# Normalization statistics as matrix products beside the router logits, in a fused attention and mixture-of-experts layer

## The chip, the cores and the metric

The kernel runs on one core of a Trainium2 chip. The metric is the device time of one execution in microseconds (us), lower is better. A core has five engines with instruction streams of their own: TensorE (PE in the profile; its weight loads are listed as PEld), VectorE (DVE), ScalarE (ACT), GpSimd (POOL) and SyncE (SP), which here issues the loop's DMAs. They wait for one another by semaphores. SBUF is the working memory, PSUM holds what TensorE writes.

## The reference

The input x is [2, 128, 256, 256] in float32: two images, 128 channels, 65,536 pixels each. One layer is computed:

```python
x = x + conv(_ln_c(x), W_qkv, W_out, rel_height, rel_width)
t = _to_tokens(x)                       # a pixel is a token of 128 channels
t = t + ffn(_ln_t(t), router_w, router_b, expert_w, expert_b)
x = _from_tokens(t, x)

def _ln_t(v, eps=1e-5):                 # _ln_c: the same over channels, eps=1e-6
    m = mean(v, -1); s = var(v, -1)
    return (v - m) / sqrt(s + eps)

def ffn(x, ...):                        # E = 8 experts, the best 2 of each token
    router_probs = softmax(x @ router_w + router_b)
    top_p, top_i = top_k(router_probs, 2)
    top_p = top_p / sum(top_p)
    expert_out = einsum('bnd,edc->bnec', x, expert_w) + expert_b
    return einsum('bnk,bnkc->bnc', top_p, gathered expert_out)
```

`conv` is attention in windows of 8 x 8 queries and 12 x 12 overlapping keys, four heads of 32 channels, with relative-position logits and a fixed mask. The mask leaves a query only the keys whose row and column have its own parity. So the image falls apart into four planes (the four parities), and each plane is attended to by itself.

## The kernel before, in words

**Layout and stages.** Channels lie on the 128 partitions, pixels along the free dimension. The image is cut into strips of 8 rows (`R`), 64 strips for both images. A strip has four planes of 4 x 128 pixels, so 512 queries each. The main loop (L707) goes over 256 planes, and eight more turns to drain. A turn n does for plane n: the scores (`scores`), the softmax and values (`attend`), the output projection (`out_project`); for plane n + 1 the projections of q, keys and values (`project`). Beside this it does for one chunk f of 512 tokens of the strip before (two rows) the statistics of the second norm and the routing (`norms`, `route`, `spread`), for one chunk c of a coming strip the statistics of the first norm (`norms`), and for the chunk whose gates were spread a turn before the eight experts' products (`Experts`).

**Order.** The loop stands under `tc.manual_schedule`, so each engine runs its instructions in the order in which the Python code emits them. The helpers are generators; every `next(...)` emits one part. A turn emits, in this order: `norm` (statistics and raw logits), the first part of `score`, `norm`'s rest, `route`'s first part, `ahead` (q of the next plane, `pq`), `ahead` (`pu`, whose transpose uT is written by DVE), `route`, the `shift` of uT (two copies and a transpose to `au`, DVE), expert product 0, the second half of the scores, `ahead` (keys, `pk`), `route`'s end, products 1 and 2, the attention's first half, `spread`, product 3, `ahead` twice (values, `pvv`), the attention's second half and its end (DVE: sT, rc, rT, o), products 4 to 7, the output projection `po` and its add to xt (L498), the product with the experts' biases (L639) and its add to xt (L640).

**The statistics before.** `stats` (L219) transposes a chunk by four PE transposes into a PSUM tile `px`, so that tokens lie on partitions, and takes `bn_stats` of each 128 x 128 block on DVE. That is done for f (`px_f`) and for c (`px_c`). `rstd` (L228) merges the halves of bn_stats by five small DVE ops and makes 1/sqrt(variance + eps) as exp(-0.5 ln(...)) by two ACT ops, followed by a correction step on DVE.

**The logits before.** `plt` (L517): four products with the router's weights `rw`, padded to 32 columns, as stationary operand and 128 tokens of the chunk moving; product t writes partitions 32t to 32t + 31. ACT copies the result to SBUF (`lT`, L525), and in `route` a PE transpose (`plg`, L548) puts tokens on partitions. A float32 product is two matmul instructions in the profile (two passes), a transpose is one.

**Gates.** `spread` transposes the gates g (`pg`, L590), copies them (ACT, `gT`), and SP writes them to DRAM (`gd`) and reads them back spread over all partitions: `rb` for the first norm, and eight `gb` of 256 KB for the experts (L598, L617), whose multiplications by xt (`xe`, L628) are shared by DVE and POOL.

**PSUM.** `mm_tile` hands out three buffers in turn (`ps_mm`), shared by px, plt, plg, pq, pu, pk, pvv, pg and po. `att` and `acc` have tiles of their own.

`ln1_now` (L289) runs `norms` for a single chunk c with nothing else around it, eight times in all (before the loop and at the start of the second image).

Of the kernel before, what the change touches and what calls it, by code (L numbers as in the profile page):

```python
# [10 lines left out]
F32 = mybir.dt.float32  # L11
AF = mybir.ActivationFunctionType
ALU = mybir.AluOpType
# [3 lines left out]
P = 128  # L17
HEADS, DH = 4, 32
E = 8
SCALE = DH ** -0.5  # L20
CONV_EPS, FFN_EPS = 1e-6, 1e-5
# [26 lines left out]
def kernel(  # L48
# [39 lines left out]
    def mm_tile(name):  # L88
        return ps_mm.tile([P, 512], F32, tag="mm", name=name)

    def ctile(shape, name):
        return const.tile(shape, F32, tag=name, name=name)
# [49 lines left out]
    def centred(w, n, name):  # L142

        pm = mm_tile(f"pm_{name}")
        nc.tensor.matmul(pm[:, :n], lhsT=onesm, rhs=w, start=True, stop=True)
        nc.vector.tensor_sub(w, w, pm[:, :n])
# [5 lines left out]
    rw = ctile([P, 32], "rw")  # L152
    nc.vector.memset(rw, 0.0)
    nc.scalar.dma_start(rw[:, 0:E], router_w)
    centred(rw, 32, "rw")
# [47 lines left out]
    epsc = ctile([P, 2 * NT], "epsc")  # L203
    nc.vector.memset(epsc[:, 0:NT], C * FFN_EPS)
    nc.vector.memset(epsc[:, NT:], C * CONV_EPS)
# [13 lines left out]
    def stats(src, st, name):  # L219


        px = mm_tile(f"px_{name}")
        for t in range(NT):
            nc.tensor.transpose(px[:, t * P : (t + 1) * P], src[:, t * P : (t + 1) * P], ident)  # L224
        for t in range(NT):
            nc.vector.bn_stats(st[:, t, :], px[:, t * P : (t + 1) * P])

    def rstd(st, eps, n, name):  # L228

        u = small.tile([P, 2 * NT], F32, tag="u", name=f"u_{name}")[:, 0:n]
        d = small.tile([P, 2 * NT], F32, tag="d", name=f"d_{name}")[:, 0:n]
        r = small.tile([P, 2 * NT], F32, tag="r", name=f"r_{name}")[:, 0:n]
        nc.vector.tensor_tensor(d, st[:, 0:n, 1], st[:, 0:n, 4], ALU.subtract)
        nc.vector.tensor_tensor(u, st[:, 0:n, 2], st[:, 0:n, 5], ALU.add)
        nc.vector.scalar_tensor_tensor(d, d, C / 4.0, d, ALU.mult, ALU.mult)
        nc.vector.tensor_tensor(u, u, eps, ALU.add)
        nc.vector.tensor_tensor(u, u, d, ALU.add)  # L240
        nc.scalar.activation(r, u, AF.Ln, scale=4.0 / C)
        nc.scalar.activation(r, r, AF.Exp, scale=-0.5)
        yield
        nc.vector.scalar_tensor_tensor(u, u, -4.0 / C, r, ALU.mult, ALU.mult)
        nc.vector.tensor_tensor(u, u, r, ALU.mult)
        yield r, u
# [158 lines left out]
    def scores(n, state):  # L405
# [35 lines left out]
        pT = work.tile([P, HEADS, HQ], F32, tag="pT", name=f"pT{n}")  # L441
# [59 lines left out]
    def norms(f, c, nm):  # L501

        st = small.tile([P, 2 * NT, 6], F32, tag="st", name=f"st{nm}", bufs=4)
        g = small.tile([P, (2 * E + 1) * NT], F32, tag="g", name=f"g{nm}")
        n0, n1 = (0 if f else NT), (2 * NT if c else NT)
        rs = lT = None
        if f:
            src = rows_of(*f)  # L510
            stats(src, st, f"f{nm}")
        if c:
            stats(ln1_src(*c), st[:, NT:, :], f"c{nm}")
        if f:
            plt = mm_tile(f"plt{nm}")
            for t in range(NT):
                nc.tensor.matmul(  # L517
                    plt[32 * t : 32 * t + 32, :P],
                    lhsT=rw,
                    rhs=src[:, t * P : (t + 1) * P],  # L520
                    start=True,
                    stop=True,
                )
            lT = work.tile([P, P], F32, tag="lT", name=f"lT{nm}")
            nc.scalar.copy(lT, plt[:, :P])  # L525
        parts = rstd(st[:, n0:], epsc[:, n0:n1], n1 - n0, nm)
        next(parts)
        yield
        r, u = next(parts)
        if f:  # L530
            rs = small.tile([P, NT], F32, tag="rs", name=f"rs{nm}")
            nc.vector.scalar_tensor_tensor(rs, u[:, 0:NT], 3.0, r[:, 0:NT], ALU.add, ALU.mult)
        if c:
            nc.vector.scalar_tensor_tensor(
                g[:, 2 * NT * E :], u[:, NT - n0 :], 3.0, r[:, NT - n0 :], ALU.add, ALU.mult
            )
        yield g, rs, lT

    def rows_of(i, k):
        return xt[i][:, 2 * k : 2 * k + 2, :].rearrange("p r c -> p (r c)")  # L540

    def route(i, k, g, rs, lT):
# [4 lines left out]
        plg = mm_tile(f"plg{nm}")  # L547
        nc.tensor.transpose(plg[:, :P], lT, ident)  # L548
        p3 = plg[:, :P].rearrange("p (t e) -> p t e", e=32)[:, :, 0:E]
        lg = small.tile([P, NT, E], F32, tag="lg", name=f"lg{nm}")  # L550
        by_e = [P, NT, E]
        nc.vector.tensor_tensor(lg, p3, rs.broadcast_to(by_e), ALU.mult)
# [153 lines left out]
    with tc.manual_schedule(engines={ET.PE, ET.DVE, ET.Activation, ET.Pool, ET.SP}):  # L706
        for n in range(n_planes + 8):  # L707
# [17 lines left out]
            next(score, None)  # L725
            made = next(norm, None)
            if f:
                g, rs, lT = made
                rout = route(*f, g, rs, lT)
            next(rout, None)  # L730
            next(ahead, None)
            next(ahead, None)
            next(rout, None)
            if n + 1 < n_planes:
                states[n + 1]["shift"]()
# [24 lines left out]
            next(attn, None)  # L760
            ex.product(4)
# [77 lines left out]
```

## Time and profile before

| | |
|---|---|
| median of 3 runs | 5080.68 us (5078.29 to 5091.52) |
| the profiled execution, its time | 5112.45 us |
| its span, first to last instruction | 5110.7 us |
| mean granted clock of TensorE | 0.987 |
| PE busy | 4958.1 us, 97% of the span |
| DVE, ACT, POOL busy | 75%, 24%, 25% |
| bytes moved by DMA | 764.01 MB, mean 149 GB/s |

The profile is a record of one execution with the start and length of each instruction. Its page lists the engines' busy time, the DMA queues, the chain of work that ended last (followed back from the last instruction) and the costliest groups of instructions. Further views are a timeline by engine, the waits (who waited for whom) and tables by stretches of time. Lengths of matmuls contain the end of the pipeline, so neighbours overlap; the distance from one start to the next is what a matmul takes of PE's time. "issue" is time in which an engine waited for nothing that the profile shows.

### The profile page before, as it was taken

Reading aid. Unit: us, or ns where it says so; the run is one execution under the profiler, and the core shown is the slowest. Engines: PE = TensorE matmul, PEld = TensorE weight load, DVE = VectorE, ACT = ScalarE, POOL = GpSimd, SP = SyncE. Lnnn points to the kernel's source line nnn. Section 1 sums busy time; section 2 is a strip of 40 time slices with the busy share of each in tenths; the row PEclk is TensorE's granted clock in tenths of the full one; section 3 lists DMA queues with packets and bytes.
Section 4 is the critical chain, followed back from the end, with each engine's and each line's share of the span. In section 5 each row is a group of like instructions: output and inputs, shape, how many; then the busy total and the mean of one; then the engine's idle time right before and its main releaser. Section 6 shows DMA issues by size and latency. Waiting matters only on the chain.

```text
span 5110.7 us, 212340 instructions
## 1 busy us (share of the span) xinstructions
PE 4958.1 (97%) x93250; PEld 2962.2 (58%) x93250; DVE 3829.9 (75%) x11636; ACT 1236.3 (24%) x3021; POOL 1283.0 (25%) x1550
## 2 busy tenths in 40 slices
PE   5999999999999999999999999999999999999998
PEld 4555655555555555555555555565555555555554
DVE  5777777777777777777777777777777777777776
ACT  2222222222222222222222222222222222222221
POOL 2222222222222222222222222222222222222221
PEclk8999999999999999999999999999999999999999
DMA  1454545445454444545445444544545545454444
GB/s 51 130 156 150 159 149 160 148 152 167 149 152 154 154 153 148 155 153 157 140 141 167 148 153 151 157 159 147 161 144 156 156 152 152 148 167 147 145 143 148
DMA packets 375143, 764.01 MB, mean 149 GB/s; under 512 B 42850, under 2 KB 61898, under 8 KB 357834
## 3 DMA queue, kind: packets, MB, share of 16 engines
q1 hardware_dynamic: 371712, 749.36, 47.2%
q8 instruction: 733, 12.01, 0.9%
q14 instruction: 192, 1.57, 0.1%
q10 hardware_dynamic: 2506, 1.07, 0.1%
HBM read 674.25 MB, written 76.01 MB: 147 GB/s over the span
## 4 chain that ended last, share of the span: by engine, by line
PE 96%; issue 2%; DVE 2%; DMA 0%; ACT 0%; POOL 0%; SPq 0%; ACTq 0%; DVEq 0%; POOLq 0%
PE acc L633 35%; PE pvv L387 9%; PE att L434 8%; PE att L465 6%; PE pk L362 5%; PE pu L350 4%; PE pq L340 4%; PE po L493 4%; PE acc L639 4%; PE att L417 3%; PE att L455 3%; PE px_f L224 2%; PE px_c L224 2%; PE plt L517 2%; PE plg L548 1%
## 5 line engine op out<-in xcount | busy, mean ns | idle before, releaser
L633 PE MATMUL acc<-xe,ew 128*128 128x512 f32 x4096 | 1961.7, 602 | 1.8 <-DVE xt L640 1.7
L628 POOL TENSOR_TENSOR xe<-xt,gb 128x512 f32<-128x512 f32 x512 | 638.0, 1267 | 3715.4 <-PE acc L633 3690.4
L633 PEld LDWEIGHTS acc<-xe,ew 128*128 128x128 f32 x4096 | 748.4, 193 | 761.1 <-issue 683.1
L628 DVE TENSOR_TENSOR xe<-xt,gb 128x512 f32<-128x512 f32 x1536 | 948.8, 685 | 15.5 <-PE acc L633 15.0
L434 PEld LDWEIGHTS att<-qs,kcol 32*64 32x64 f32 x32768 | 430.0, 130 | 257.8 <-issue 257.1
L387 PEld LDWEIGHTS pvv<-wt,xcol 128*128 128x128 f32 x4096 | 498.7, 192 | 119.2 <-issue 119.0
L498 DVE TENSOR_TENSOR xt<-po,xt 128x512 f32<-128x512 f32 x256 | 177.2, 692 | 494.9 <-PE po L493 494.9
L434 PE MATMUL att<-qs,kcol 32*64 32x32 f32 x32768 | 466.4, 224 | 55.3 <-issue 54.8
L387 PE MATMUL pvv<-wt,xcol 128*128 128x128 f32 x4096 | 500.6, 275 | 0.0
L525 ACT COPY lT<-plt 128x128 f32<-128x128 f32 x256 | 68.1, 266 | 1716.5 <-PE plt L517 1716.5
L465 PEld LDWEIGHTS att<-pT,vv 64*32 64x32 f32 x32768 | 376.2, 106 | 69.1 <-issue 1.3
L475 DVE STREAM_TRANSPOSE sT<-att 128x512 f32<-128x512 f32 x256 | 183.5, 717 | 305.0 <-PE att L465 305.0
L394 ACT COPY vv<-pvv 128x512 f32<-128x512 f32 x512 | 300.1, 586 | 454.9 <-PE pvv L387 454.9
L465 PE MATMUL att<-pT,vv 64*32 64x32 f32 x32768 | 399.9, 199 | 0.2 <-issue 0.2
L282 POOL TENSOR_TENSOR xn<-xt,rb 128x512 f32<-128x512 f32 x248 | 372.8, 1503 | 61.9 <-DMA rb<-gd 61.9
L442 ACT ACTIVATE pT<-att 128x1024 f32<-128x1024 f32 x256 | 262.5, 1025 | 179.1 <-PE att L434 179.1
L362 PE MATMUL pk<-xn,wt 128*128 128x512 f32 (+2 forms) x528 | 291.7, 637 | 0.0
L493 PE MATMUL po<-o,wt 128*128 128x512 f32 x512 | 265.7, 601 | 16.9 <-DVE o L485 16.9
L340 PE MATMUL pq<-xn,wt 128*128 128x512 f32 x512 | 271.8, 613 | 6.8 <-DVE lg L556 2.6
L329 DVE STREAM_TRANSPOSE au<-auT 128x512 f32<-128x512 f32 x256 | 269.9, 1054 | 8.8
L350 PE MATMUL pu<-xn,wrel 128*128 128x512 f32 x512 | 271.2, 611 | 2.3 <-issue 1.4
L639 PE MATMUL acc<-ge,eb 128*128 128x512 f32 x512 | 261.5, 592 | 0.0
(2951 smaller groups left out, 5364.4 us busy)
## 6 DMA issues: line engine op xcount, KB each, us to landing
gb<-gd SPq DMA_DIRECT2D x2048, 256.0 KB
xt<-in_x_dram SPq DMA_DIRECT2D x64, 1024.0 KB
out_dram<-xt SPq DMA_DIRECT2D x64, 1024.0 KB
rb<-gd SPq DMA_DIRECT2D x248, 256.0 KB
gd<-gT SPq DMA_DIRECT2D x244, 34.0 KB
ge<-gd SPq DMA_DIRECT2D x256, 16.0 KB
ew<-in_L_ffn_expert_w_dram ACTq DMA_DIRECT2D x1, 512.0 KB
gd<-gT SPq DMA_DIRECT2D x12, 32.0 KB
```

Source lines behind the costliest of these rows:

```text
L282: eng.tensor_tensor(xn[i % 2][:, :, :, k, 1 : PC + 1], ln1_src(i, k).rearrange("p (y j x) -> p y x j", y=2, x=2), rb.rearrange("p (y j x) ...
L340: nc.tensor.matmul(pq, lhsT=wq, rhs=inner, start=True, stop=True)
L350: nc.tensor.matmul(pu, lhsT=wrel, rhs=inner, start=True, stop=True)
L362: nc.tensor.matmul(pk[:, : m * PC], lhsT=wk, rhs=xp[:, part[0] : part[0] + m, 1 : PC + 1], start=True, stop=True,)
L387: nc.tensor.matmul(pv[:, t * P : (t + 1) * P], lhsT=xl[:, t0 + t].rearrange("p a k -> p (a k)"), rhs=wv, start=True, stop=True,)
L394: nc.scalar.copy(vv[:, t0 : t0 + 4, :].rearrange("p t c -> p (t c)"), pv)
L434: nc.tensor.matmul(sc[rows, h, 32 * t : 32 * t + 32], lhsT=kk[hp, half * HP + t, :], rhs=qs[hp, m0 : m0 + 2].rearrange("p m a s -> p (m a ...
L465: nc.tensor.matmul(av[hp, half, 32 * t : 32 * t + 32], lhsT=vv[rows, t, hp], rhs=pT[rows, h, 32 * t : 32 * t + 32], start=True, stop=True,)
L493: nc.tensor.matmul(po, lhsT=wo, rhs=state["o"].rearrange("p f z -> p (f z)"), start=True, stop=True)
L628: eng.tensor_tensor(self.xe[e], self.src, self.gb.pop(e), ALU.mult)
L633: nc.tensor.matmul(self.acc, lhsT=ew[:, e, :], rhs=self.xe.pop(e), start=(e == 0), stop=False)
L639: nc.tensor.matmul(self.acc, lhsT=eb, rhs=self.ge, start=False, stop=True)
```

## The change

The transposes, bn_stats and half of `rstd` go. For each chunk ACT writes the squares of the raw values (`sq0`, `sq2`). The router's weights become four blocks of 32 columns: block 0 has the logits' weights, and block j has in column E + j the value 1/C (block 0 has its own too). Four times four products are accumulated in the same tile `plt`: block 0 with f, block 1 with f's squares, block 2 with c, block 3 with c's squares. So the columns after the eight logits hold the mean and the mean square of f and of c. After the copy `lT` and the transpose `plg`, which moves from `route` to `norms`, DVE reads the moments from PSUM, and `rstd` forms the variance as mean square less squared mean.

In the order of a turn: the squares are emitted first, then the first part of the scores, then the 16 products and `lT`, then q's projection (`pq`), then `plg` and `rstd`, then `route` and `pu`. The `shift` moves from before expert product 0 to after the attention's end (o), before product 4. pT and the squares have one buffer each.

```diff
--- before.py
+++ after.py
@@ -149,10 +149,14 @@
     nc.scalar.dma_start(ew, expert_w.rearrange("e d c -> d e c"))
     for e in range(0, E, 4):
         centred(ew[:, e : e + 4, :].rearrange("p e c -> p (e c)"), 512, f"ew{e}")
-    rw = ctile([P, 32], "rw")
+
+
+    rw = ctile([P, 4, 32], "rw")
     nc.vector.memset(rw, 0.0)
-    nc.scalar.dma_start(rw[:, 0:E], router_w)
-    centred(rw, 32, "rw")
+    nc.scalar.dma_start(rw[:, 0, 0:E], router_w)
+    centred(rw[:, 0, 0:E], E, "rw")
+    for j in range(4):
+        nc.vector.memset(rw[:, j, E + j : E + j + 1], 1.0 / C)
     rb = ctile([P, E], "rb")
     nc.scalar.dma_start(rb, router_b.partition_broadcast(P))
 
@@ -200,9 +204,9 @@
         nc.gpsimd.memset(auT[i][:, :, :, KR + 6 : KR + 7], NEG)
 
 
-    epsc = ctile([P, 2 * NT], "epsc")
-    nc.vector.memset(epsc[:, 0:NT], C * FFN_EPS)
-    nc.vector.memset(epsc[:, NT:], C * CONV_EPS)
+    epsc = ctile([P, 2, NT], "epsc")
+    nc.vector.memset(epsc[:, 0], FFN_EPS)
+    nc.vector.memset(epsc[:, 1], CONV_EPS)
 
 
     xn, xcol, kcol = [], [], []
@@ -216,34 +220,25 @@
         nc.gpsimd.memset(kcol[i], 0.0)
 
 
-    def stats(src, st, name):
-
-
-        px = mm_tile(f"px_{name}")
-        for t in range(NT):
-            nc.tensor.transpose(px[:, t * P : (t + 1) * P], src[:, t * P : (t + 1) * P], ident)
-        for t in range(NT):
-            nc.vector.bn_stats(st[:, t, :], px[:, t * P : (t + 1) * P])
-
-    def rstd(st, eps, n, name):
-
-
-
-
-        u = small.tile([P, 2 * NT], F32, tag="u", name=f"u_{name}")[:, 0:n]
-        d = small.tile([P, 2 * NT], F32, tag="d", name=f"d_{name}")[:, 0:n]
-        r = small.tile([P, 2 * NT], F32, tag="r", name=f"r_{name}")[:, 0:n]
-        nc.vector.tensor_tensor(d, st[:, 0:n, 1], st[:, 0:n, 4], ALU.subtract)
-        nc.vector.tensor_tensor(u, st[:, 0:n, 2], st[:, 0:n, 5], ALU.add)
-        nc.vector.scalar_tensor_tensor(d, d, C / 4.0, d, ALU.mult, ALU.mult)
-        nc.vector.tensor_tensor(u, u, eps, ALU.add)
-        nc.vector.tensor_tensor(u, u, d, ALU.add)
-        nc.scalar.activation(r, u, AF.Ln, scale=4.0 / C)
+    def rstd(p4, k0, k1, name):
+
+
+
+        u, r = (
+            small.tile([P, 2, NT], F32, tag=v, name=f"{v}_{name}")[:, k0:k1] for v in ("u", "r")
+        )
+        mean, sq = (
+            p4[:, :, E + 2 * k0 + j : E + 2 * k1 : 2].rearrange("p t k -> p k t") for j in range(2)
+        )
+        nc.vector.tensor_copy(r, mean)
+        nc.vector.tensor_tensor(u, r, r, ALU.mult)
+        nc.vector.scalar_tensor_tensor(u, u, -1.0, sq, ALU.mult, ALU.add)
+        nc.vector.scalar_tensor_tensor(u, u, 0.0, epsc[:, k0:k1], ALU.max, ALU.add)
+        nc.scalar.activation(r, u, AF.Ln, scale=4.0)
         nc.scalar.activation(r, r, AF.Exp, scale=-0.5)
-        yield
-        nc.vector.scalar_tensor_tensor(u, u, -4.0 / C, r, ALU.mult, ALU.mult)
+        nc.vector.scalar_tensor_tensor(u, u, -4.0, r, ALU.mult, ALU.mult)
         nc.vector.tensor_tensor(u, u, r, ALU.mult)
-        yield r, u
+        return r, u
 
     def ln_rows(i):
 
@@ -438,7 +433,7 @@
                         start=False,
                         stop=(t == HP - 1),
                     )
-        pT = work.tile([P, HEADS, HQ], F32, tag="pT", name=f"pT{n}")
+        pT = work.tile([P, HEADS, HQ], F32, tag="pT", name=f"pT{n}", bufs=1)
         nc.scalar.activation(pT, att[:, :, 0:HQ], AF.Exp)
         state.update(att=att, pT=pT)
         yield
@@ -502,54 +497,54 @@
 
 
 
-        st = small.tile([P, 2 * NT, 6], F32, tag="st", name=f"st{nm}", bufs=4)
         g = small.tile([P, (2 * E + 1) * NT], F32, tag="g", name=f"g{nm}")
-        n0, n1 = (0 if f else NT), (2 * NT if c else NT)
-        rs = lT = None
-        if f:
-            src = rows_of(*f)
-            stats(src, st, f"f{nm}")
-        if c:
-            stats(ln1_src(*c), st[:, NT:, :], f"c{nm}")
-        if f:
-            plt = mm_tile(f"plt{nm}")
+        srcs = []
+        for j, src in ((0, f and rows_of(*f)), (2, c and ln1_src(*c))):
+            if src is None:
+                continue
+            sq = work.tile([P, CH], F32, tag=f"sq{j}", name=f"sq{j}{nm}", bufs=1)
+            nc.scalar.activation(sq, src, AF.Square)
+            srcs += [(j, src), (j + 1, sq)]
+        yield
+        plt = mm_tile(f"plt{nm}")
+        for j, src in srcs:
             for t in range(NT):
                 nc.tensor.matmul(
                     plt[32 * t : 32 * t + 32, :P],
-                    lhsT=rw,
+                    lhsT=rw[:, j],
                     rhs=src[:, t * P : (t + 1) * P],
-                    start=True,
-                    stop=True,
+                    start=(j == srcs[0][0]),
+                    stop=(j == srcs[-1][0]),
                 )
-            lT = work.tile([P, P], F32, tag="lT", name=f"lT{nm}")
-            nc.scalar.copy(lT, plt[:, :P])
-        parts = rstd(st[:, n0:], epsc[:, n0:n1], n1 - n0, nm)
-        next(parts)
-        yield
-        r, u = next(parts)
+        lT = work.tile([P, P], F32, tag="lT", name=f"lT{nm}")
+        nc.scalar.copy(lT, plt[:, :P])
+        yield
+        plg = mm_tile(f"plg{nm}")
+        nc.tensor.transpose(plg[:, :P], lT, ident)
+        p4 = plg[:, :P].rearrange("p (t e) -> p t e", e=32)
+        k0, k1 = (0 if f else 1), (2 if c else 1)
+        r, u = rstd(p4, k0, k1, nm)
+        rs = None
         if f:
             rs = small.tile([P, NT], F32, tag="rs", name=f"rs{nm}")
-            nc.vector.scalar_tensor_tensor(rs, u[:, 0:NT], 3.0, r[:, 0:NT], ALU.add, ALU.mult)
+            nc.vector.scalar_tensor_tensor(rs, u[:, 0], 3.0, r[:, 0], ALU.add, ALU.mult)
         if c:
             nc.vector.scalar_tensor_tensor(
-                g[:, 2 * NT * E :], u[:, NT - n0 :], 3.0, r[:, NT - n0 :], ALU.add, ALU.mult
+                g[:, 2 * NT * E :], u[:, 1 - k0], 3.0, r[:, 1 - k0], ALU.add, ALU.mult
             )
-        yield g, rs, lT
+        yield g, rs, p4
 
     def rows_of(i, k):
         return xt[i][:, 2 * k : 2 * k + 2, :].rearrange("p r c -> p (r c)")
 
-    def route(i, k, g, rs, lT):
+    def route(i, k, g, rs, p4):
 
 
         nm = f"{i}_{k}"
         rs = rs.unsqueeze(2)
-        plg = mm_tile(f"plg{nm}")
-        nc.tensor.transpose(plg[:, :P], lT, ident)
-        p3 = plg[:, :P].rearrange("p (t e) -> p t e", e=32)[:, :, 0:E]
         lg = small.tile([P, NT, E], F32, tag="lg", name=f"lg{nm}")
         by_e = [P, NT, E]
-        nc.vector.tensor_tensor(lg, p3, rs.broadcast_to(by_e), ALU.mult)
+        nc.vector.tensor_tensor(lg, p4[:, :, 0:E], rs.broadcast_to(by_e), ALU.mult)
         nc.vector.tensor_tensor(lg, lg, rb.unsqueeze(1).broadcast_to(by_e), ALU.add)
         mx = small.tile([P, NT, 1], F32, tag="mx2", name=f"mx2{nm}")
         nc.vector.tensor_reduce(mx, lg, AX.X, ALU.max)
@@ -723,16 +718,14 @@
 
             next(norm, None)
             next(score, None)
+            next(norm, None)
+            next(ahead, None)
             made = next(norm, None)
             if f:
-                g, rs, lT = made
-                rout = route(*f, g, rs, lT)
+                rout = route(*f, *made)
             next(rout, None)
             next(ahead, None)
-            next(ahead, None)
             next(rout, None)
-            if n + 1 < n_planes:
-                states[n + 1]["shift"]()
             ex.product(0)
             next(score, None)
             next(ahead, None)
@@ -758,6 +751,8 @@
             next(ahead, None)
             next(attn, None)
             next(attn, None)
+            if n + 1 < n_planes:
+                states[n + 1]["shift"]()
             ex.product(4)
             ex.product(5)
             for e in (5, 7):
```

## The prediction

> **What bounds the kernel now.** I read the page first: engines, DMA queues and the chain that ended last.
>
> ```profile
> span 5110.7 us, 212340 instructions
> PE 4958.1 (97%) x93250; PEld 2962.2 (58%) x93250; DVE 3829.9 (75%) x11636; ACT 1236.3 (24%) x3021; POOL 1283.0 (25%) x1550
> ...
> q8 instruction: 733, 12.01, 0.9%
> ...
> PE 96%; issue 2%; DVE 2%; DMA 0%; ACT 0%; POOL 0%; SPq 0%; ACTq 0%; DVEq 0%; POOLq 0%
> ```
>
> TensorE (PE) carries 96% of the chain, "issue" 2%. So the change is worth what it does to PE's own time, to those issue gaps, and to any new PE wait. Next the timeline of PE over one undisturbed plane (start, length, work):
>
> ```profile
> 2727.86 0.60 PE L224 MATMUL px_f<-ident,xt 128*128 128x128 f32 x4
> 2728.29 0.60 PE L224 MATMUL px_c<-ident,xt 128*128 128x128 f32 x4
> 2728.82 0.43 PE L517 MATMUL plt<-xt,rw 128*32 128x128 f32 x8
> 2729.18 0.69 PE L417 MATMUL att<-au,keys 32*64 32x128 f32 x32
> 2729.67 0.90 PE L434 MATMUL att<-qs,kcol 32*64 32x32 f32 x64
> 2730.50 0.33 PE L548 MATMUL plg<-ident,lT 128*128 128x128 f32 x1
> 2730.66 1.02 PE L340 MATMUL pq<-xn,wt 128*128 128x512 f32 x2
> 2731.53 1.02 PE L350 MATMUL pu<-xn,wrel 128*128 128x512 f32 x2
> 2732.39 1.02 PE L633 MATMUL acc<-xe,ew 128*128 128x512 f32 x2
> 2733.34 0.86 PE L434 MATMUL att<-qs,kcol 32*64 32x32 f32 x64
> ...
> 2738.09 0.30 PE L590 MATMUL pg<-ident,g 128*68 128x128 f32 x1
> ...
> 2746.91 0.60 PE L224 MATMUL px_f<-ident,xt 128*128 128x128 f32 x4
> ```
>
> Lengths include the pipeline's end; what a piece costs is the distance between starts. The plane takes 2746.91 - 2727.86 = 19.05 us, the median of all planes, with no hole. Third, PE's waits, and the chain in order of time and the table of stretches around one of them:
>
> ```profile
> PE att L434 <- issue: 54.8, 54, 2.7
> ```
>
> ```profile
> 2527.67 0.60 PE att L417 x30
> 2528.27 0.55 PE att L434 x32
> 2528.82 2.66 issue
> 2531.48 0.34 PE att L434 x11
> ...
> 2532.23 1.71 PE pq L340 x2
> ```
>
> ```profile
> 2528.70:2531.50 2.80, 0.14 (x15) 0.02 (x4) 1.31 (x10) 0.42 (x2) 0.00 (x0) 1.00 1.01 369
> 2531.50:2535.30 3.80, 3.80 (x19) 1.83 (x19) 0.76 (x4) 0.81 (x2) 0.00 (x0) 0.55 0.20 74
> ```
>
> PE stops in the middle of the scores with nothing to wait for, while the DMA share (second last column) is 1.01; afterwards the granted clock (third last) is 0.55. That plane took 23.78 us, 4.7 too many.
>
> **What the issue gaps are.** Queue q8 moved 12.01 MB in 733 packets, 16 KB each. PE has 2 x 93250 instructions and about 1170 semaphore ones: 256 for each packet. Counting PE's records, every gap in the scores falls on the same count modulo 256 (193 or 194). So PE's instructions come in blocks of 256, and a gap is a block that came late. Its packet's records agree: PE resumes 1.2 to 1.6 us after the end (here the packet ran 2529.30 to 2530.23). When DMA is idle, a packet starts about 1.2 us after PE's sequencer enters the block before (the records fit best if it runs at most 48 instructions ahead). But 3 us after pg starts, SP has begun to issue rb and eight gb of 256 KB; the packet records show the 16 DMA engines full from 4 to 12.5 us (odd planes) or 14 us (even) after pg, and a block asked for at 3.3 us starts 8.3 us later, at 9 us some 3 to 5 later. The scores that follow use up 192 instructions in 1.3 us, at 10.1 us after pg (2738.09 to 2748.23). In all, from 170 to 5015 us, 68 such gaps idle 68 us, 80 counted from start to start; 14 of the longest bring a half-clock stretch of 3.4 us.
>
> [...]
>
> **The change, part by part.**
>
> *Removed on PE:* eight transposes, px_f 2728.29 - 2727.86 = 0.43 and px_c 0.53 us, and the present plt, 0.36: 1.32 us a plane.
>
> *Added on PE:* plt of four products by four column tiles, each in two passes: 32 matmuls in 8 passes. In the records of the present plt the four tiles of a pass start within 20 ns, the second pass starts 0.133 us after the first (its weights load meanwhile), and the next work 0.22 us after that. In keys (L417), also 128 columns a pass, later passes come every 0.109 us. So 0.133 + 6 x 0.109 + 0.22 = 1.01 us. The last acc (L639) is now followed by small tiles: acc before att costs 0.95, before pvv 0.86, so +0.09. Net 1.01 + 0.09 - 1.32 = -0.22 us. Bounds: 8 x 0.109 = 0.87 gives -0.36; four times today's plt, 1.42, gives +0.19. I take -0.22, nearest to a row with the same columns per pass. Times 248 planes that have both halves: -55 us (-89 to +47).
>
> [...] The present plt shows the second loads starting 26 ns after the first matmul, so the row decides.
>
> *New wait, plt for ScalarE's squares.* A square is [128 x 512]; the nearest rows, the vv and qs copies, take 0.59 us. ACT is idle 6.7 us before lT and the rows are there, so both are done before the scores. Where pl is 0 the last row arrives with the xt add (L498, done 0.1 us into the plane): squares end at 1.35, and plt wants them at 1.6 and 2.1. Nothing. Behind the squares on ACT wait only lT and qs.
>
> *plg, now after pq.* lT ends about 0.6 us after plt's last matmul starts; pq covers 0.86. Nothing; without that cover up to 0.6 us a plane. plg's PSUM buffer is po's, free at 0.1 us.
>
> *The statistics' chain* (DVE and ACT) now starts at plg. In plane time: plg ends 3.5; four small DVE ops 0.8; Ln and Exp 0.5; four ops 0.65; logits 0.9 (6.4); uT 0.65; cmp, cmp, rank 1.25; five gate ops 1.1: g at 9.4, as now (2718.2 against px at 2708.79). pg wants it at 9.9. The eight bn_stats (1.76 us) and the shift (1.35 us), moved behind o, no longer stand before it. Cover 0.5 us; what is over would cost its length on PE. pT's Exp on ACT comes behind lg's, 0.3 us later, with 1 us to spare.
>
> *Shift moved.* DVE is idle 1.94 us before L498 (waiting for po), the shift takes 1.35, and au is ready 1 us before keys. Nothing behind it on DVE waits longer. SP's issues keep their order and their distance from pg.
>
> *DVE's saving* buys nothing: PE hardly waits for DVE in planes.
>
> *The ends:* eight single rows before and beside the loop (L294) gain a square, lT and plg on a serial path (+1.2) and lose four bn_stats and an op (-0.9), and four last planes are serial too: +10 us (0 to 20).
>
> *The issue gaps.* PE gets 8 x 2 fewer and 12 x 2 x 2 more instructions: +32 a plane, 33 more blocks, at the dense place. And the scores start 8.9 us after pg and not 10.1: deeper in the full DMA, with plt's 64 dense instructions behind them. A boundary in the scores or plt, whose block was asked for after gb began, gets it no earlier, but PE is there 1.2 us sooner. By hand: a block asked for 3.3 to 9 us after pg starts at 11.6 to 13 and is there 2.3 us later, at 14 to 15; the new order needs it at 8.9 to 11.3 if the boundary lies in the scores or plt, so such a gap is near 3 us or more; today's scores end at 11.5, the longest gap there is 2.7 us, and a boundary past them meets 2.8 us of slow products first. I laid the block rule over PE's order, with the starting delays of the packet records at the same distance from pg. Set so that it gives 76 us and 13 gaps over 1.9 us for the present order (records: 80 and 13 to 15), it gives an estimated 150 to 220, middle 180, and 32 to 58 over 1.9 us for the new order. So +100 us (0 to +140), and 30 more half-clock stretches. One costs about 1.5 us more (4.7 - 2.9 in the plane above, less for shorter ones): +45 (0 to +65).
>
> **Sum,** against the profiled 5112.45 us: -55 + 10 + 100 + 45 = +100, so 5212. The median of the runs shown is 5080.68, 31.8 less. If all of that were gaps and their clock (about 105 us), the gaps would weigh 0.7 there; if none, 1. I take 0.8 of 145 = 116: 5080.68 - 55 + 10 + 116 = **5152 us**.
>
> **Rivals.**
> 1. *Faster: the gaps don't grow.* PE's -55 and the ends' +10 remain: 5036 us. For it: the gaps come from where block boundaries happen to fall, and the new order may spread the gb issue differently; in plain PE time the change gains. Against: gaps sit exactly at the scores, which come earlier. It decides where gaps and clock together grow by less than 45 / 0.8 = 56 us.
> 2. *Half growth:* 5036 + 58 = 5094, no measurable change.
> 3. *Products don't overlap:* plt at 1.42 us or more, +102 us on the forecast: 5254. Against: plt's records of today.
> 4. *Boundaries lock.* 728 + 32 instructions and some semaphore ones come near 768 = 3 x 256, so boundaries may sit still from plane to plane: by the same estimate 50 to 340 us of gaps, 5010 to 5300.
> 5. *The change doesn't do what it says:* Square forces table loads (one today, 1.28 us) twice a plane; the second would delay g to 10.7, PE by 0.8 x 250 = +200: 5350.
>
> **Chances.** Forecast 0.54, rival 1 0.22, rival 2 0.10, rival 3 0.06, rival 4 0.06 (a third of it faster), rival 5 0.02. Range 5028 to 5240: from rival 1 with some of plt's lower bound to the forecast with the gaps' and the ends' upper bounds (5152 + 0.8 x 60 + 10 = 5210) and part of plt's; the likeliest case alone spans 5100 to 5235. A measurement tells 0.3% (15 us) from no change: faster 0.24, same 0.11, slower 0.65.
>
> **What would show it.** Right: plt's 32 matmuls start to start near 1.0 us; an undisturbed plane of 18.8; q8 near 766 packets; issue gaps at L434 and now plt and pq totalling over 100 us, on one count modulo 256, and more half-clock stretches. Wrong: undisturbed planes above 19.05 (plt, or PE waiting for lT, sq or g), gaps unchanged, or an ACT table load in the loop.

## The result, and the profile after

The changed kernel takes 5513.9 us in the median (5507.57 to 5523.81, 4 runs) against 5086.1 us (5078.29 to 5095.87, 4 runs) for the kernel before: ratio 1.0842, 95% interval 1.0813 to 1.087. The forecast of 5152 us had the sign, but the time is far above its range (5028 to 5240). The profiled execution took 5517.84 us. Lines of the page after (its line numbers are 5 smaller than before in most of the code):

```profile
span 5516.1 us, 218900 instructions
PE 5006.7 (91%) x97358; PEld 2920.5 (53%) x97358; DVE 3968.9 (72%) x9324; ACT 1506.5 (27%) x3545; POOL 1283.7 (23%) x1550
...
q8 instruction: 766, 12.55, 0.9%
...
PE 66%; DVE 28%; issue 5%; DMA 0%; ACT 0%; POOL 0%; DVEq 0%; SPq 0%; ACTq 0%; POOLq 0%
...
L319 DVE COPY auT<-uT 128x96 f32<-128x96 f32 x512 | 661.2, 1331 | 0.0
```

VectorE has 2312 instructions fewer (2048 bn_stats and one small operation in each of 268 `rstd`, against four more memsets at the start) and is busy 139 us longer. It now holds 28% of the chain that ended last (before: 2%). The last line says why. The two copies of `shift`, the same instruction as before on the same shape, take 1331 ns each. In the kernel before their group reads:

```profile
L324 DVE COPY auT<-uT 128x96 f32<-128x96 f32 x512 | 81.8, 203 | 0.2
```

What that does to TensorE stands in PE's waits of the kernel after (total us, times, longest):

```profile
PE att L412 <- DVE au L324: 257.9, 248, 1.5
PE plt L512 <- issue: 112.8, 35, 4.6
PE att L429 <- issue: 33.4, 46, 2.5
```

The first wait did not exist before: in 248 of the 256 planes the scores wait about 1.04 us for `au`. The other two are issue gaps, which before were 54.8 us in the scores. The timeline of one plane boundary of the kernel after (start, length, work, idle time before it):

```profile
2725.14 2.50 POOL L623 TENSOR_TENSOR xe<-xt,gb 128x512 f32<-128x512 f32 x2 [14.81 <-PE acc L628]
...
2725.90 0.69 DVE L480 TENSOR_TENSOR o<-att,rT 128x512 f32<-128x512 f32 x1
2726.51 2.66 DVE L319 COPY auT<-uT 128x96 f32<-128x96 f32 x2
...
2727.60 1.51 POOL L277 TENSOR_TENSOR xn<-xt,rb 128x512 f32<-128x512 f32 x1
...
2728.33 1.02 PE L634 MATMUL acc<-ge,eb 128*128 128x512 f32 x2
...
2729.20 1.05 DVE L324 STREAM_TRANSPOSE au<-auT 128x512 f32<-128x512 f32 x1
...
2730.40 0.70 PE L412 MATMUL att<-au,keys 32*64 32x128 f32 x32 [1.06 <-DVE au L324]
```

GpSimd multiplies from 2725.14 to 2727.64 and again from 2727.60 to 2729.11. The copies begin at 2726.51, inside the first of these, and end at 2729.17, just after the second. The transpose of 1.05 us follows, so `au` is there at 2730.25; PE, done with its last product, waited 1.06 us.

### The profile page after: what moved, and what is told of

Read it like the earlier page. It is cut to its first block, busy times and chain, and to the rows that moved or that the text cites. A ratio compares the mean times of both kernels' runs of the same rounds, so it can differ in the third digit from the quotient of the medians.

```text
span 5516.1 us, 218900 instructions
## 1 busy us (share of the span) xinstructions
PE 5006.7 (91%) x97358; PEld 2920.5 (53%) x97358; DVE 3968.9 (72%) x9324; ACT 1506.5 (27%) x3545; POOL 1283.7 (23%) x1550
## 4 chain that ended last, share of the span: by engine, by line
PE 66%; DVE 28%; issue 5%; DMA 0%; ACT 0%; POOL 0%; DVEq 0%; SPq 0%; ACTq 0%; POOLq 0%
PE acc L628 17%; DVE auT L319 12%; PE pvv L382 8%; PE att L429 7%; PE att L460 6%; PE pq L335 6%; PE plt L512 5%; PE pk L357 5%; DVE au L324 5%; PE pu L345 4%; DVE sT L470 3%; DVE rT L475 3%; DVE o L480 3%; PE att L412 3%; PE att L450 3%
## 5 line engine op out<-in xcount | busy, mean ns | idle before, releaser
L623 POOL TENSOR_TENSOR xe<-xt,gb 128x512 f32<-128x512 f32 x512 | 640.3, 1272 | 4117.0 <-PE acc L628 4091.3
L623 DVE TENSOR_TENSOR xe<-xt,gb 128x512 f32<-128x512 f32 x1536 | 950.5, 687 | 13.4 <-PE acc L628 12.9
L319 DVE COPY auT<-uT 128x96 f32<-128x96 f32 x512 | 661.2, 1331 | 0.0
L412 PE MATMUL att<-au,keys 32*64 32x128 f32 x8192 | 181.0, 282 | 257.9 <-DVE au L324 257.9
L506 ACT ACTIVATE sq<-xt 128x512 f32<-128x512 f32 x504 | 291.2, 626 | 436.8 <-DVE xt L493 436.8
L277 POOL TENSOR_TENSOR xn<-xt,rb 128x512 f32<-128x512 f32 x248 | 371.8, 1499 | 69.0 <-DMA rb<-gd 69.0
L412 PEld LDWEIGHTS att<-au,keys 32*64 32x64 f32 x8192 | 125.6, 132 | 463.6 <-PE acc L634 362.0
L335 PE MATMUL pq<-xn,wt 128*128 128x512 f32 x512 | 322.8, 714 | 9.7 <-issue 9.7
L345 PE MATMUL pu<-xn,wrel 128*128 128x512 f32 x512 | 289.3, 648 | 6.8 <-issue 6.8
L512 PE MATMUL plt<-sq,rw 128*32 128x128 f32 x4032 | 223.6, 281 | 74.7 <-issue 74.4
```

The source lines that it names most:

```text
L277: eng.tensor_tensor(xn[i % 2][:, :, :, k, 1 : PC + 1], ln1_src(i, k).rearrange("p (y j x) -> p y x j", y=2, x=2), rb.rearrange("p (y j x) ...
L319: nc.vector.tensor_copy(auT[n % 2][:, :, :, 6 * j : 6 * j + 6], bass.AP(shifted.tensor, shifted.offset, dims),)
L335: nc.tensor.matmul(pq, lhsT=wq, rhs=inner, start=True, stop=True)
L345: nc.tensor.matmul(pu, lhsT=wrel, rhs=inner, start=True, stop=True)
L412: nc.tensor.matmul(sc[rows, h].rearrange("p (t w z) -> p t w z", w=2, z=16)[:, :, w], lhsT=keys[hp, turn, w], rhs=au[hp, half * NP + w : ( ...
L512: nc.tensor.matmul(plt[32 * t : 32 * t + 32, :P], lhsT=rw[:, j], rhs=src[:, t * P : (t + 1) * P], start=(j == srcs[0][0]), stop=(j == srcs ...
```

## The experiments

**First question: the wait for au.** Theory: the copies are slow because GpSimd is at work beside them in their new place. Four kernels change only the shift; all four ran beside the kernel before at 5113.4 us (5106.88 to 5124.84, 7 runs).

*The changed kernel with the shift put back to where it was:*

```diff
             next(rout, None)
+            if n + 1 < n_planes:
+                states[n + 1]["shift"]()
             ex.product(0)
...
-            if n + 1 < n_planes:
-                states[n + 1]["shift"]()
             ex.product(4)
```

> The changed kernel with the shift back at its old place, before expert product 0, where POOL is idle. Theory P (the two auT copies are held up by POOL's multiplications, and au then comes late for the scores): the copies fall from 1331 ns to about 0.20 us, the wait of L412 for au (about 1.08 us in each of 249 planes, 270 us) goes; the block gaps, 199 us in the changed kernel, stay or grow a little, because the scores then start 1.1 us sooner after pg. 5514 - 270 + 0 to 60 = 5240 to 5310 us, still 3 to 4.5% above the kernel before. Rival R (the late blocks are the main cost, and the wait for au only fills time in which PE would have waited for instructions anyway): the gaps grow by what the wait gives back, 5400 us or more.

Measured 5311.93 us (5300.62 to 5341.49), ratio 1.0396 (1.0355 to 1.0436), 2 us above the expected range. The copies take 202 ns and `att <- au` is gone. The issue gaps stay (77.1 us at plt, 60.8 at the scores), and another wait came:

```profile
PE pg L585 <- DVE g L578: 103.5, 168, 3.1
```

Here the shift, 2 x 0.20 + 1.05 = 1.45 us, stands in front of the gate operations on VectorE, whose chain begins later in the new order. An undisturbed plane is 19.50 us, 0.62 more than the 18.88 of the kernel without either wait (below). So the change had a reason to move the shift; the place it got costs more.

*The kernel before with the shift put to the late place and nothing else changed:*

```diff
-            if n + 1 < n_planes:
-                states[n + 1]["shift"]()
             ex.product(0)
...
+            if n + 1 < n_planes:
+                states[n + 1]["shift"]()
             ex.product(4)
```

> The kernel before with nothing but the shift moved to its late place. Theory P: the copies take 1.2 to 1.5 us there too, though no statistics changed; DVE ends the shift about 1.6 us into the next plane. The scores start 1.3 us into the plane and wait little for au, but the add of po (L498) stands behind the shift on DVE, and plt takes po's PSUM buffer: PE should wait some 1.0 to 1.4 us a plane, at plt and the scores together, +250 to +350 us: 5340 to 5440. Rival R: without the squares and the 16 products the move costs nothing that can be measured, copies 0.2 us, 5086 +- 20.

Measured 5289.97 us (5271.44 to 5296.38), ratio 1.0336 (1.0313 to 1.036). The move alone makes the copies 1327 ns. The cost is less than expected, and the wait stands elsewhere: px comes before the scores here and hides part of au's lateness, while the xt add (L498), which stands behind the shift on VectorE, frees po's PSUM buffer late. Waits of this kernel:

```profile
PE plt L517 <- DVE xt L498: 110.0, 179, 0.6
PE px_f L224 <- DVE xt L498: 78.0, 62, 1.6
```

*The changed kernel with the copies in another form,* the shift still late. First as a tensor_tensor with two SBUF inputs:

```diff
-            nc.vector.tensor_copy(
-                auT[n % 2][:, :, :, 6 * j : 6 * j + 6],
-                bass.AP(shifted.tensor, shifted.offset, dims),
+            moved = bass.AP(shifted.tensor, shifted.offset, dims)
+            nc.vector.tensor_tensor(
+                auT[n % 2][:, :, :, 6 * j : 6 * j + 6], moved, moved, ALU.max
             )
```

> The changed kernel, shift at its late place, but the two copies written as an elementwise maximum of the source with itself (tensor_tensor). Theory P, read from the trace: tensor_tensor on DVE (xe, o) takes 0.69 us beside POOL's multiplication as without it, so the copies should take 0.2 to 0.3 us and au come in time: 5240 to 5310. [...] Rival Q (the copies are slow for their own access pattern at that place, not for their kind): also 1.3 us and 5514.

Measured 5561.03 us (5524.48 to 5575.01), ratio 1.0861 (1.082 to 1.0902). The expectation missed: the instruction is as slow as the copy. The row that it went by had been misread. In the changed kernel `xe` on VectorE, two SBUF inputs, touched GpSimd's work in only 5 of its 1536 instructions; the two that lay well inside it took 1753 and 1758 ns, the others some 685. `o`, which does run beside GpSimd (691 ns), has one of its inputs in PSUM. Then on ScalarE:

```diff
-            nc.vector.tensor_copy(
+            nc.scalar.copy(
```

> The changed kernel with the two auT copies on ScalarE (ACT), the transpose to au stays on DVE at its late place. Theory P: ACT copies take about 0.25 us, no waiting for POOL, and are done long before o; au comes in time: 5230 to 5310. If the transpose itself or the late place on DVE were the cause, L412 would still wait for au: 5400 or more.

Measured 5276.24 us (5273.14 to 5287.35), ratio 1.0319 (1.0302 to 1.0336). And, in the second set (kernel before 5110.93 us, 5086.82 to 5125.07, 13 runs), as a VectorE instruction with one SBUF input that is no copy (if the form decides, it was expected to take 0.2 to 0.4 us beside busy GpSimd, at a ratio of 1.025 to 1.04):

```diff
-            nc.vector.tensor_copy(
-                auT[n % 2][:, :, :, 6 * j : 6 * j + 6],
-                bass.AP(shifted.tensor, shifted.offset, dims),
+            nc.vector.tensor_reduce(
+                auT[n % 2][:, :, :, 6 * j : 6 * j + 6].unsqueeze(4),
+                bass.AP(shifted.tensor, shifted.offset, dims + [[1, 1]]),
+                AX.X,
+                ALU.max,
             )
```

> The changed kernel with the two shift copies written as VectorE tensor_reduce(max) over an axis of one element: still late in the turn, still on VectorE, still from SBUF to SBUF, but with one SBUF input and not as a copy. In the changed kernel a copy took 1331 ns beside the multiplications of GpSimd, and as a tensor_tensor with two SBUF inputs 1362 ns. [...] Rival B (any VectorE instruction that reads and writes SBUF alone is held up by GpSimd): still 1.2 us or more, au late as in the changed kernel, ratio 1.075 to 1.09.

Measured 5308.61 us (5292.31 to 5313.99), ratio 1.0388 (1.0352 to 1.0423). It is a little slower than the ScalarE kernel (1.0319), and its issue gaps are longer (123.1 us at plt against 100.8). The groups of these three kernels, in this order:

```profile
L320 DVE TENSOR_TENSOR auT<-uT 128x96 f32<-128x96 f32 x512 | 677.7, 1362 | 0.0
```

```profile
L319 ACT COPY auT<-uT 128x96 f32<-128x96 f32 x512 | 118.7, 283 | 1.9 <-DVE uT L347 1.9
```

```profile
L319 DVE TENSOR_REDUCE auT<-uT 128x96 f32<-128x96 f32 x512 | 103.7, 244 | 0.0
```

The two forms on VectorE have the same data, the same place and the same neighbours on GpSimd: 1362 ns with two SBUF inputs, 244 ns with one. So it is not the access pattern or the place. The ScalarE copies (283 ns) start earlier, before `o`, and all 512 ran with GpSimd idle; they show that the late copies were the cost, not what ScalarE would do beside GpSimd. In the last two kernels `att <- au` no longer shows among PE's waits. Sorted by what GpSimd did meanwhile, the 512 copies of the kernel after are 505 with GpSimd busy (median 1207 ns) and 7 with GpSimd idle (199 to 210 ns); in the kernel before, all 512 ran with GpSimd idle. The tensor_tensor: median 1256 ns and about 251 ns. The tensor_reduce: 244 ns in both. So in these runs GpSimd holds up two forms of VectorE instruction, the copy and the tensor_tensor with two SBUF inputs, and not the tensor_reduce; what sets the forms apart, the runs do not show. The hold lasts until GpSimd's instruction is done: 504 of the 505 copies end 61 to 182 ns (median 66) after the end of one. GpSimd's own times hardly move (this multiplication took 1267 ns before and 1272 ns after).

**Second question: what remains without the wait for au.** Ratio 1.03, though the undisturbed plane is now 18.88 us against 19.05 before. Theory: PE's instruction blocks (766 packets of 16 KB on queue q8) come late behind the gb transfers. One such gap in the kernel after, in its chain in order of time and its table of stretches (after the length come the busy times of PE, PEld, DVE, ACT and POOL; the last three columns are the granted clock, the DMA share and GB/s):

```profile
1123.88 0.79 PE plt L512 x23
1124.67 4.44 issue
1129.11 0.80 PE plt L512 x9
```

```profile
1119.00:1124.40 5.40, 4.37 (x125) 2.64 (x124) 4.44 (x5) 0.00 (x0) 3.07 (x4) 1.00 0.88 267
1124.40:1129.10 4.70, 0.27 (x11) 0.01 (x2) 0.00 (x0) 0.00 (x0) 0.00 (x0) 0.73 0.54 204
1129.10:1133.00 3.90, 3.89 (x14) 1.85 (x14) 0.66 (x4) 0.89 (x3) 0.00 (x0) 0.50 0.01 4
```

PE stops in the middle of plt for 4.44 us with nothing to wait for, after a stretch with a DMA share of 0.88, and goes on at a granted clock of 0.50. The one packet of the instruction queue q8 there ran from 1126.70 to 1127.74, and PE went on 1.37 us after its end. To test the theory, the transfers were taken away, in the changed kernel with the copies on ScalarE:

```diff
+            if e not in fixed:
+                fixed[e] = ctile([P, NT * P], f"gbfix{e}")
+                nc.sync.dma_start(fixed[e], to_all(self.gd, E + e))
+            self.gb[e] = fixed[e]
-            self.gb[e] = gates.tile([P, NT * P], F32, tag="gb", name=f"gb{nm}", bufs=8)
-            nc.sync.dma_start(self.gb[e], to_all(self.gd, E + e))
```

> The changed kernel with the copies on ScalarE, and the gate multipliers gb loaded once for the first chunk and used for all: left out are eight transfers of 256 KB a plane, so the experts' weights of the output are those of the first chunk. With the loads, this kernel had an undisturbed plane of 18.88 us, issue gaps of some 190 us in all and 191 us at half clock. Theory A (the gaps are blocks of PE instructions that come late behind the gb transfers): gaps under 30 us, half clock under 30 us, planes at 18.9 us, 4960 to 5010 us, ratio 0.97 to 0.98. Rival B (the gaps come from the number of PE instructions at the scores and plt alone): gaps and half clock stay, ratio 1.02 to 1.04.

Measured 4979.1 us (4977.41 to 4983.3), ratio 0.9749 (0.972 to 0.9779). PE executes the same 97358 matmuls at the same places, and of its gaps there is left:

```profile
PE att L429 <- issue: 2.7, 4, 1.7
...
PE plt L512 <- issue: 2.1, 7, 0.6
```

The number of PE instructions alone makes no gap, and the stretches at half clock go with the gaps (191.1 us with gb, 3.4 without, counted from 170 us to the last planes). The same edit in the kernel before (beside 5105.9 us, 5090.1 to 5128.06, 7 runs):

> The kernel before with the gate multipliers gb of the first chunk used for all chunks: the eight transfers of 256 KB a plane are left out, so the experts' weights of the output are those of the first chunk. It is the counterpart of the run with the copies on ScalarE and without these transfers, which took 4979.1 us. Theory A (in the kernel before, too, late blocks behind gb cost some 102 us with their half clock, and all that the products themselves save on TensorE is 0.17 us a plane): 5005 to 5025 us, 26 to 46 above its counterpart, ratio 0.979 to 0.984. Rival B (the products save the 55 us that the prediction counted): 5030 us or more.

Measured 5007.13 us (5005.41 to 5009.83), ratio 0.9805 (0.9775 to 0.9834): 28 us above its counterpart, which ran in another set. That is all the change is worth when neither the shift nor the transfers are in the way.

**Third question: can the transfers stay, at other times?** In the kernel before, five of the eight are issued from ScalarE's queue, spread over the next turn; the changed kernel with ScalarE copies got the same edit. Its lines are shown; in the kernel before the same calls stand at the corresponding places, the first two between `norm` and the scores and between the two calls of `ahead`:

```diff
-        nxt.fetch(e)
+        if e in (0, 4, 6):
+            nxt.fetch(e)
...
             next(norm, None)
+            nxt.fetch(1, nc.scalar)
             next(ahead, None)
+            nxt.fetch(2, nc.scalar)
...
             next(score, None)
+            nxt.fetch(3, nc.scalar)
             next(ahead, None)
+            nxt.fetch(5, nc.scalar)
+            nxt.fetch(7, nc.scalar)
```

> The kernel before with the same eight gb transfers, but spread: three stay on SyncE where they are, five are issued from ScalarE's queue at places through the following turn. Theory A: the 59 us of issue gaps and their half clock fall to a third or less, nothing else changes: ratio 0.98 to 0.99. Rival B: the issue of a transfer costs ScalarE so much time that its exponentials come late and TensorE waits for them: ratio 1.00 to 1.03.

> The changed kernel with the copies on ScalarE and the gb transfers spread as in the run before this one. Theory A: gaps and half clock mostly gone, the shorter plane of 18.88 us remains: ratio 0.97 to 0.985, below both kernels. Rival B (blocks come late wherever a transfer runs, or ScalarE becomes late): ratio 1.00 to 1.04.

The kernel before with spread transfers: 5032.06 us (5030.46 to 5034.91), ratio 0.9852 (0.9822 to 0.9882); its issue gaps fall from 59 to 19 us and its half-clock stretches from 51 to 10 us. The changed one: 5087.66 us (5081.04 to 5098.51), ratio 0.9964 (0.9945 to 0.9984), above Theory A's range and below Rival B's. Its gaps are still 53.4 us at plt. Those over 1.3 us come in every other plane, where SP's transfers (the 1 MB loads and stores of x among them) fill the DMA engines until 10.6 us after pg, while the scores begin 8.9 us after pg. So two more of the transfers were moved and two of the others put later, only expert 0 staying on SP (against the run just shown):

```diff
-        if e in (0, 4, 6):
+        if e == 0:
             nxt.fetch(e)
...
             next(norm, None)
-            nxt.fetch(1, nc.scalar)
+            ex.fetch(4, nc.scalar)
             next(ahead, None)
-            nxt.fetch(2, nc.scalar)
+            ex.fetch(6, nc.scalar)
             made = next(norm, None)
             if f:
                 rout = route(*f, *made)
+            nxt.fetch(1, nc.scalar)
             next(rout, None)
             next(ahead, None)
             next(rout, None)
+            nxt.fetch(2, nc.scalar)
```

> The changed kernel with the copies on ScalarE and the gb transfers spread further: only expert 0 stays on SyncE, the other seven are issued from ScalarE's queue between the scores and the next pg. In the run with five moved, the remaining gaps (53 us, 37 at plt) came in every other plane, where SyncE's transfers still filled the DMA engines until 10.6 us after pg; the scores begin at 8.9 us. Theory A (only transfers that stand before the block make it late): these gaps go, 4985 to 5020 us, ratio 0.975 to 0.983, below the kernel before with spread transfers (0.985). Rival B (seven transfers of 256 KB do not fit between the scores and the next pg, so multiplications after pg come late, or blocks needed at the attention's output come late instead): 5060 us or more, ratio 0.99 to 1.03.

Measured 5024.3 us (5022.68 to 5026.0), ratio 0.9838 (0.9802 to 0.9874; this run and the next beside 5105.9 us). It is just above Theory A's range: the gaps at plt fall from 53.4 to 31.0 us and are not gone:

```profile
PE plt L512 <- issue: 31.0, 28, 2.1
```

This version beats both kernels, but by the spread transfers: against the kernel before with the same idea (0.9852) the difference lies within the intervals. The last kernel also puts pq before the scores, and pu between plt and plg:

```diff
             next(norm, None)
+            next(ahead, None)
             next(score, None)
             next(norm, None)
...
             next(rout, None)
-            next(ahead, None)
             next(rout, None)
```

> The same as the run with seven transfers moved, and the product pq issued before the scores, pu between plt and plg. The dense stretch of keys, qs and plt is then between two sparse ones, and its first block is asked for 0.9 us later after pg. Theory A: as that run or up to 20 us less, ratio 0.970 to 0.983. Rival B (scores 0.9 us later make the exponential of pT, and with it the attention's products, late): TensorE waits for pT at L450 or for g at L585, ratio 0.99 to 1.03.

Measured 5205.55 us (5200.86 to 5210.93), ratio 1.0193 (1.0161 to 1.0225). Rival B holds. The gaps at plt stay (31.8 us), and two waits come:

```profile
PE att L450 <- ACT pT L437: 91.0, 245, 2.9
PE pg L585 <- DVE g L578: 58.1, 247, 3.1
```

The scores, and plt with plg behind them, now start 0.83 us later after pg (the scores at 9.74 us instead of 8.91), and an undisturbed plane costs 0.64 us more (19.52 us): the chains from the scores and from plt have less cover than that.

## Why the prediction was wrong

The runs split the difference of the profiled spans, 5516.1 - 5110.7 = 405.4 us, into three parts. Each span is of one execution, and those of the kernel before lie up to some 40 us apart within one set, so a part is good to some tens of us:

| part | from which spans | us | forecast |
|---|---|---|---|
| shift beside GpSimd, au late | 5516.1 - 5285.6 (copies on ScalarE) | +230.5 | 0 |
| late blocks and half clock | (5285.6 - 4975.6) - (5110.7 - 5005.7) = 310.0 - 105.0 | +205.0 | +145, weighed to +116 |
| products and ends | 4975.6 - 5005.7 (no gb in either) | -30.1 | -45 |

The split depends on its order. In the kernel after, the wait for au itself is 257.9 us; but it also starts the scores later (10.02 us after pg, 8.91 with ScalarE copies), and its issue gaps are 163.4 us instead of 195.3. So the first part is smaller than the wait, and the second larger than in the kernel after.

**The step that failed** is "Shift moved. DVE is idle 1.94 us before L498 (waiting for po), the shift takes 1.35, and au is ready 1 us before keys." Its cost was set at nothing. The hole on VectorE was there, but the shift's length was taken from its old place, where GpSimd was idle. In the hole GpSimd multiplies, as the timeline of before already has it:

```profile
2723.81 2.49 POOL L628 TENSOR_TENSOR xe<-xt,gb 128x512 f32<-128x512 f32 x2 [13.51 <-PE acc L633]
2726.26 1.50 POOL L282 TENSOR_TENSOR xn<-xt,rb 128x512 f32<-128x512 f32 x1
2727.20 0.69 DVE L498 TENSOR_TENSOR xt<-po,xt 128x512 f32<-128x512 f32 x1 [1.94 <-PE po L493]
```

The hole is the 1.94 us before L498, and GpSimd is busy all through it. In the new place the shift takes 2 x 1.33 + 1.05 = 3.7 us. Au is 1.04 us late instead of 1 us early. The prediction asked what stands behind the shift on its own engine, and not what runs beside it on another.

**The issue gaps** were right in mechanism and mis-sized. On the copies-on-ScalarE kernel, from 170 us to the last planes, they are 195.3 us in 127 gaps (the same count in before: 58.6 in 56), +137, with 191.1 us in 48 half-clock stretches (51.2 in 15): 33 more against the 30 forecast. Counted from start to start, as the forecast counted them, the gaps are about 235 us against about 83 (13 and 3 without gb): the transfers' share grows by some 142 us where the forecast had +100. This is the term that was too small. What is left of the 205 us, some 63, is an estimate of what the half clock cost, forecast 45. Which part of the gaps' estimate fell short, the places of the blocks or their delays, the runs do not show. The gaps in the scores, plt, pq and pu fall on one count of PE's instructions modulo 256 (193 or 194), as forecast, and PE goes on 1.2 to 1.6 us after the late packet's end. Single gaps reach 5.4 us (at plt, in the kernel with the tensor_tensor); without gb the longest at plt is 0.6 us, at the scores 1.7. The weight of 0.8, which was to bring the profiled execution down to the median, made the term smaller still. In medians, which come from three sets, the term is (5276.24 - 4979.1) - (5105.9 - 5007.13) = 198 us, so no weight was due.

**The products** came out near the forecast. plt's 32 matmuls take 1.01 us from start to start (forecast 1.01), q8 moved 766 packets (forecast 766). An undisturbed plane is 18.88 us: 0.17 saved and not 0.22, since pq, now between plt's small tiles and plg, takes 0.97 instead of 0.86, and plg 0.11 instead of 0.165. The ends cost what was forecast within what can be told: 0.17 x 249 = 42 us less in the planes, 30 less in all, so some 12 us (forecast 10).

**Of the rivals** none happened. Rival 3 (products that do not overlap) and rival 5 (table loads: there is one of 1.28 us, as before) are refuted. Rivals 1 and 2 fall with the gaps, which grew by more than the forecast and not less. Rival 4 (boundaries that sit still) had its premise nearly right. In the records of the kernel after, a plane has 765 to 767 PE instructions, semaphore ones included, in 97% of the loop's planes, so the block boundaries move by only some 2 a plane (before: 732 or 733, so by 35 or 36). Planes with more than 2 us of gaps therefore come in bunches, 18 of them from plane 35 to 62, 17 from 182 to 204 and one later (before: 5, scattered). But over the loop the boundaries move by some 520 instructions, two rounds of 256, so the total is an average over all positions and not the luck of one. That the gate chain's cover was thin was seen; the kernel with the shift put back shows it (0.62 us a plane when 1.45 us stand before it). The kernel with ScalarE copies says what the forecast would have met without its failed step: slower by 163 us (5276.24 against 5113.4 in its set, ratio 1.0319), where +71 was forecast. On the 5086.1 us beside the result that is some 5248 us, just above the upper end of the range, because of the gaps.

## What to carry to other kernels

When an instruction is moved into an idle hole of its engine, look at the timeline of the other engines in that hole, and take its length from a row with the same neighbour; here the form of the VectorE instruction decided how long it took beside GpSimd (tensor_reduce 244 ns, copy 1331 ns, for the same data). Where PE's instructions are dense after a burst of DMA, look for PE's own blocks among the transfers: here issuing five of the eight transfers later was worth 1.5% (0.9852, 0.9822 to 0.9882) without touching the arithmetic, more than the 28 us that the change itself is worth. Removing work from an engine that nobody waits for (VectorE, 2312 instructions) bought nothing that can be seen: PE's own 0.17 us a plane, less the ends, accounts for the 30 us.

## What the runs showed of the hardware

- A VectorE instruction that is blocked by GpSimd counts as busy in the profile: 661 us of "work" for copies that need 82. VectorE's idle time and waits do not show it. What does is the mean of the same group in two kernels, or the spread within one group (198, 1207 and 1546 ns as shortest, median and longest).
- Each copy is held for the GpSimd instruction at work: in the timeline above the first ends with L623, the second with L277, 2.66 us for two copies of 0.2 us. GpSimd did not slow down (its multiplication by gb took 1272 ns, 1267 before).
- Other VectorE work beside GpSimd was not slowed: the transpose to `au` took 1045 ns beside GpSimd in the kernel after and 1054 ns with GpSimd idle in the one before (medians), and the multiplication `o`, with one input in PSUM and one in SBUF, ran beside GpSimd in both at 691 ns. `tensor_reduce` took 244 ns with GpSimd busy or idle.
- Without the gb transfers PE runs 97358 matmuls with issue gaps of 2.7 and 2.1 us in all at the two dense places (scores and plt), and with them up to 124.4 us at plt (the tensor_tensor kernel): the dense code cost no more than that while DMA moved a mean of 46 GB/s, against 139 in the kernel after.
